# Two attention and expert layers on one core: the second attention's side work placed over whole batches, and two normalizations handed from VectorE to ScalarE

## Chip, core and metric

The kernel runs on one core of a Trainium2 chip. The metric is device time in microseconds (us) of the whole program. TensorE is written PE, VectorE is DVE, ScalarE is ACT, GpSimd is POOL, and SP is the engine that issues most of the DMAs.

## What is computed

Two layers, each a cross attention followed by a mixture of experts, over x of 4 batches, 512 rows and 256 columns, with a context of 4 x 1601 rows. Everything is fp32.

```
x = x + attention0(ctx, layernorm(x))        # 8 heads of 128, context and latents as keys
x = x + experts0(layernorm(x))               # 8 experts, top 2, capacity 512 per expert, gelu (tanh)
x = x + attention1(ctx, layernorm(x))        # 8 heads of 32: q from x, k and v from ctx
x = x + experts1(layernorm(x))               # 8 experts, top 2 by threshold, softmax weights, gelu (erf)

layernorm(x) = (x - mean(x)) / sqrt(var(x) + 1e-5)        # over the 256 columns
attention1:  softmax((q @ Wq.T) (ctx @ Wk.T).T * 32**-0.5) @ (ctx @ Wv.T)
experts1:    logits = x @ Wr + br; keep the two largest; w = softmax(kept)
             out = sum over e of w[e] * (gelu(x @ W1[e] + b1[e]) @ W2[e] + b2[e])
```

## The kernel before

The program has four stages, which follow each other on the one core.

1. First attention, from the start to about 1600 us of the profiled execution.
2. First experts. All eight experts are computed for the first half of their slots and then for the second half (`all_experts`, line 1304). Beside the second half runs `keys_next` (line 1374): keys and values of batch 1 for the second attention, the sum of batch 0's expert results into x (`add_collected`, line 347), the normalized queries of batch 0 (`queries`, line 1128) and its first maxima. `all_experts` takes one piece of this generator at three places of each expert.
3. Second attention, lines 1430 to 1704. There are 16 units, four to a batch: half of the heads (o) by half of the queries (f). A unit goes over the 1601 keys in 13 steps of 128, and the loop at line 1672 takes the steps two at a time. Such a pair of steps is called a pair below, and the steps are numbered 0 to 207, 52 to a batch. In each pair stand, in this order: the scores of two key blocks (`weights`, PE) and their exponentials (line 1476, ACT); the product with the values (`weigh`, PE); one piece of the row maxima of the next unit (`maxima`, PE, and two DVE reductions at line 1205 that read PSUM); the sums of the exponentials (line 1481, DVE); and then whatever the table `at` holds for these steps.
4. Second experts (from line 1709): 8 tiles of 256 rows, one for each expert, and then 13 further tiles from `SURE`, of which the last is short (128 rows). `hidden` is the first layer, `results` the second with the add into the output by an indirect DMA on POOL. The output adds follow one another.

The side work of stage 3 is put into `at` by hand. For batch b, with s0 = 52 b:

- `route2(b - 1)` (line 406): normalizes the finished rows of batch b - 1 for the second experts, chooses experts, counts places, adds the bias product and scatters the rows. It is a generator, and `place` takes one piece of it at each given offset from s0.
- `collect(b + 1)` and `add_collected(b + 1)`: gather the first experts' results on POOL, and add them to x on DVE.
- `queries(b + 1)`: row moments on DVE, a square root on ACT (line 144), five small DVE operations (`ln_scale`), four DVE operations that normalize 128 rows each (line 159), transposes, and two products on PE.
- `projected` (line 1639), for b of 1 and 2: 15 pieces that make keys and values of batch b + 1 on PE, one every two steps, copied out of PSUM by ACT.

PE, DVE, ACT and POOL keep the written order in stage 3 (`in_order(*computing)`, line 1662). SP does not, and neither do the other stages outside the first attention's opening, where a list scheduler orders the instructions; there an instruction is only held by `keep_in_program_order`. In stage 3 all score products, all maxima, and most of the side products share one PSUM pool of three buffers (`c_ps_s`, line 1434); the first side product of a pair takes `c_ps_m`.

[...]

Of the kernel before, what the change touches and what calls it, by code (L numbers as in the profile page):

```python
# [16 lines left out]
P = 128  # L17
# [57 lines left out]
def xattn_ffn_twice(ctx: ExitStack, tc: tile.TileContext, a: dict, out: bass.AP):  # L75
# [61 lines left out]
        nc.vector.tensor_scalar(ve, mv[:, :, 1], EPS, None, ALU.add)  # L137
        return ve

    def ln_root(pool, mv, n, ve=None):  # L140
# [3 lines left out]
        nc.scalar.activation(rs, ve, AF.Sqrt)  # L144
        return ve, rs

    def ln_scale(pool, mv, n, root=None):
# [258 lines left out]
    def route2(b, two, psum, tag, first=0, n=NT):  # L406
# [7 lines left out]
        ve = ln_variance(two, mv, n)  # L414
        yield

        root = ln_root(two, mv, n, ve)
        yield
        mv, rs = ln_scale(two, mv, n, root)
        yield  # L420
        for t in range(n):
            nc.vector.tensor_scalar(
                pay[:, t, :D],
                xb[:, t, :],
                mv[:, t, 0:1],
                rs[:, t : t + 1],
                ALU.subtract,
                ALU.mult,
            )
# [698 lines left out]
    def queries(b, qT):  # L1128
        xn = soon.tile([P, NT, D], F32, tag="xn", name="xn")
        mv = ln_moments(turns, x[b], NT, some=())  # L1130
        for i in range(NT):
            ln_moments(turns, x[b], NT, mv=mv, some=(i,))
            if i + 1 < NT:
                yield
        ve = ln_variance(turns, mv, NT)
        yield

        root = ln_root(turns, mv, NT, ve)
        yield
        mv, rs = ln_scale(turns, mv, NT, root)  # L1140
        for i in range(NT):
            ln_apply(xn, x[b], mv, rs, i)
            if i in (0, NT - 1):
                yield
        xnT = soon.tile([P, DC, S], F32, tag="xnT", name="xnT")
        transposed(banks["beside"], "s", xnT, xn, NT)
        yield
        for o in range(DC):
            ps = banks["beside"].tile([P, 512], F32, tag="s", name="ps_q1")
            for c in range(DC):  # L1150
                nc.tensor.matmul(
                    ps,
                    lhsT=wT[:, 0, c, o * P : (o + 1) * P],
                    rhs=xnT[:, c, :],
                    start=c == 0,
                    stop=c == DC - 1,
                )
            nc.scalar.activation(qT[:, o, :], ps, AF.Copy, scale=DH1**-0.5)
            yield
# [82 lines left out]
    with ExitStack() as st:  # L1242
# [187 lines left out]
    with ExitStack() as st:  # L1430
# [175 lines left out]
        for u in range(1, n_units):  # L1606

            put(NM * u - 7, lambda u=u: negated(u))
            put(NM * u - 5, lambda u=u: to_row(u))
            put(NM * u - 12, lambda u=u: load_queries(u))  # L1610
        for b in range(B):
            s0 = per_batch * b
            if b:
                put(s0 - 10, lambda b=b: load_keys(b, 0))
                put(s0, lambda b=b: load_keys(b, 1))

                beside = (4, 8, 10, 18, 20, 22, 24, 28, 30, 32, 34, 36, 38, 40, 42, 44, 46)
                bare = (4, 8, 10, 12, 12, 14, 14, 16, 18, 20, 22, 24, 26, 28, 30, 32, 34)
                steps = beside if b + 1 < B else bare
                place(s0, route2(b - 1, one, side, "s"), (*steps, *range(steps[-1] + 2, 54, 2), *range(54, 62)))  # L1620
            if b + 1 < B:
                put(s0 + 1, lambda b=b: begin(b + 1))
                got, steps = collect(b + 1)

                for k, f in enumerate(steps):
                    put(max(s0 - 28, 0) + 1 + k, f)
                for t in range(NT):
                    put(
                        s0 + 10 + 2 * t,
                        lambda b=b, got=got, t=t: add_collected(b + 1, got, (t,)),  # L1630
                    )

                def later(b=b):
                    yield from queries(b + 1, qTs[b + 1])

                place(s0, later(), range(12, 32, 2))
            if 1 <= b and b + 1 < B:

                def projected(b=b):
                    *kv, steps = keys_values(side, "s", b + 1, nc.scalar.copy)  # L1640
                    kvs.append(kv)
                    yield
                    for f in steps:
                        f()
                        yield
# [63 lines left out]
    with ExitStack() as st:  # L1709
# [61 lines left out]
            turned_rows(rows, xT, tp)  # L1771
            return xT

        def hidden(w, xT, two=two):
# [345 lines left out]
```

## Time and profile before

| | |
|---|---|
| median of 3 runs | 2819.07 us (2818.01 to 2824.54) |
| the profiled execution | 2825.64 us |
| its span in the profile | 2823.9 us, so 1.7 us lie around it |
| PE busy | 2711.7 us, 96% |
| DVE busy | 1458.4 us, 52% |
| ACT busy | 939.3 us, 33% |
| second attention | from 1914.4 to about 2524 us |
| second experts | from about 2524 us to the end |

Busy time counts an instruction's own duration, and a matmul that runs at a lower clock counts as longer, so a busy PE can still be slow. The granted clock is the share of full speed that PE's clock had in a stretch. A wait names the engine and line that came last before the instruction could begin. The averages hide that the stages have different limits: in the second attention DVE is busy for most of the time, in the experts it hardly is.

### The profile page before, as it was taken

What the parts mean: (1) busy time and instruction counts of PE and PEld (TensorE: products, weight loads), DVE (VectorE), ACT (ScalarE), POOL (GpSimd) and SP (SyncE); (2) the same over time, 40 slices, a digit from 0 to 9 for tenths busy, and PEclk for the clock granted to TensorE, in tenths of its full rate; (3) what the DMA queues carried; (4) which work ended last, traced back from release to release, by engine and by line L of the source; (5) the groups of instructions that cost most, each with busy time, mean ns of one, the idle gap of its engine ahead of it and who ended that gap; (6) DMA issues with size and microseconds to landing.
All of it is one profiled execution on the core that took longest, in us unless ns stands there. A gap on an engine that the chain in (4) does not pass through costs nothing. (4 is left out here: it accounts for less than half of the span.)

```text
span 2823.9 us, 35983 instructions
## 1 busy us (share of the span) xinstructions
PE 2711.7 (96%) x13566; PEld 1853.8 (66%) x13566; DVE 1458.4 (52%) x2307; ACT 939.3 (33%) x1362; POOL 262.4 (9%) x292
## 2 busy tenths in 40 slices
PE   6999999999999999999999999998999998889998
PEld 3667676666666676666676687874454454458887
DVE  6444556544476445455444412137887878872111
ACT  4323234232333233332332211114444444442221
POOL 0000000100001000001000001001110202022542
PEclk9999999999999999999999999999999999999999
DMA  5444343433343433334434555525621111025573
GB/s 172 116 112 116 97 113 86 111 95 92 93 120 89 106 96 95 96 82 107 98 91 125 166 174 172 173 80 156 176 68 40 38 30 56 31 77 188 163 219 103
DMA packets 196435, 311.95 MB, mean 110 GB/s; under 512 B 43319, under 2 KB 117368, under 8 KB 193560
## 3 DMA queue, kind: packets, MB, share of 16 engines
q1 hardware_dynamic: 157512, 227.52, 29.4%
q0 software_dynamic: 14160, 46.31, 5.6%
q10 hardware_dynamic: 24576, 35.68, 4.9%
q8 instruction: 111, 1.82, 0.3%
q14 instruction: 76, 0.62, 0.1%
HBM read 111.73 MB, written 51.34 MB: 58 GB/s over the span
## 5 line engine op out<-in xcount | busy, mean ns | idle before, releaser
L852 DVE TENSOR_REDUCE top<-ps_s 128x1 f32<-128x2113 f32 x128 | 301.8, 2358 | 587.3 <-PE ps_s L844 587.3
L881 PE MATMUL ps_o<-pT,v 128*128 128x256 f32 x2176 | 521.6, 381 | 0.5 <-DVE inv L859 0.5
L844 PE MATMUL ps_s<-kT,qT 128*128 128x512 f32 (+1 forms) x1280 | 489.0, 526 | 5.8 <-ACT attn L858 5.8
L881 PEld LDWEIGHTS ps_o<-pT,v 128*128 128x128 f32 x2176 | 409.9, 191 | 115.2 <-issue 68.4
L858 ACT ACTIVATE attn<-ps_s,top 128x2113 f32<-128x2113 f32 x128 | 259.0, 2024 | 478.8 <-DVE top L852 435.3
L844 PEld LDWEIGHTS ps_s<-kT,qT 128*128 128x128 f32 x1280 | 241.6, 190 | 252.4 <-issue 237.2
L873 DVE STREAM_TRANSPOSE pT<-swapped 128x2176 f32<-128x2176 f32 x128 | 312.4, 2440 | 33.4 <-DMA swapped<-attn 22.7
L1205 DVE TENSOR_REDUCE tops<-ps_s 128x2 f32<-128x1024 f32 (+1 forms) x224 | 238.3, 1105 | 107.4 <-PE ps_s L1194 106.3
L793 PE MATMUL ps_k<-kvin,wkv 128*128 128x512 f32 (+1 forms) x640 | 262.7, 533 | 3.8 <-DVE mv_g L731 2.1
L1463 PE MATMUL ps_w<-asked,keyed 64*128 64x256 f32 (+1 forms) x1664 | 227.8, 408 | 35.0 <-DVE tops L1205 35.0
L827 PE MATMUL ps_v<-wkv,kvin 128*128 128x256 f32 x1088 | 254.6, 381 | 1.3 <-ACT v L834 1.3
L1476 ACT ACTIVATE pT<-ps_w 128x1024 f32<-128x1024 f32 x192 | 189.8, 1022 | 154.1 <-PE ps_w L1463 138.5
L827 PEld LDWEIGHTS ps_v<-wkv,kvin 128*128 128x128 f32 x1088 | 204.7, 190 | 36.8 <-ACT v L834 6.3
L1463 PEld LDWEIGHTS ps_w<-asked,keyed 64*128 64x128 f32 (+1 forms) x1664 | 151.6, 189 | 113.4 <-DVE tops L1205 55.6
L1481 DVE TENSOR_TENSOR sum<-sum,pT 128x1024 f32<-128x1024 f32 x176 | 214.7, 1220 | 13.5 <-PE ps_o L1490 4.9
L806 ACT ACTIVATE kT<-ps_k,bqk 128x512 f32<-128x512 f32 (+1 forms) x160 | 96.8, 620 | 262.9 <-PE ps_k L793 122.4
L793 PEld LDWEIGHTS ps_k<-kvin,wkv 128*128 128x128 f32 x640 | 115.8, 191 | 77.6 <-issue 67.0
L834 ACT COPY v<-ps_v 128x512 f32<-128x512 f32 x144 | 79.7, 560 | 216.6 <-PE ps_v L827 148.3
L1194 PE MATMUL ps_s<-kv,qT 32*128 32x512 f32 (+1 forms) x1024 | 137.0, 561 | 8.8 <-DVE tops L1205 5.1
L1279 PE MATMUL ps_h<-sxT,w 128*128 128x256 f32 x512 | 116.1, 384 | 4.0 <-ACT hT L1286 4.0
L1293 PE MATMUL ps_y<-w,hT 128*128 128x256 f32 x512 | 116.8, 384 | 0.0
L1279 PEld LDWEIGHTS ps_h<-sxT,w 128*128 128x128 f32 x512 | 97.9, 192 | 20.8 <-ACT hT L1286 4.8
(306 smaller groups left out, 2516.1 us busy)
## 6 DMA issues: line engine op xcount, KB each, us to landing
swapped<-attn SPq DMA_DIRECT2D x1536, 68.0 KB
swapped<-attn ACTq DMA_DIRECT2D x512, 68.0 KB
w<-in_w_dram SPq DMA_DIRECT2D x32, 1024.0 KB
rows_b<-empty SPq DMA_DIRECT2D x36, 530.0 KB
w_e<-in_wall_dram SPq DMA_DIRECT2D x5, 2052.0 KB
cw<-in_ctxT_dram SPq DMA_DIRECT2D x4, 1601.0 KB
keyed<-kv SPq DMA_DIRECT2D x32, 200.1 KB
ctx_b<-in_ctx_dram SPq DMA_DIRECT2D x3, 1536.0 KB
```

What stands on the lines that cost most here:

```text
L793: nc.tensor.matmul(ps[:, :n], lhsT=wkv[:, c, hs], rhs=kvin[:, c, : NB - 1, k, :] if k < 4 else kvin[:, c, NB - 1, :, :], start=c == 0, sto ...
L827: nc.tensor.matmul(ps[:, k, :], lhsT=flat_kvin[c][:, j * P : (j + 1) * P], rhs=wkv[:, c, cols], start=c == 0, stop=c == DC - 1,)
L844: nc.tensor.matmul(flat[:, j0 : j0 + n], lhsT=qT[:, t * P : (t + 1) * P], rhs=kT[:, j0 : j0 + n], start=True, stop=True,)
L852: nc.vector.tensor_reduce(top, flat[:, :L], AX.X, ALU.max, negate=True)
L858: nc.scalar.activation(attn[:, :L], flat[:, :L], AF.Exp, bias=top, accum_out=total)
L873: nc.vector.transpose(pT[:, :, k * P : (k + 1) * P].rearrange("p c (a i) -> p a c i", a=4), swapped.rearrange("p a (c i) -> p a c i", i=32),)
L881: nc.tensor.matmul(ps, lhsT=v[:, j - parts[part][0], (h % 2) * DH0 : (h % 2 + 1) * DH0], rhs=pT[:, j, :], start=j == 0, stop=j == NB - 1,)
L1205: nc.vector.tensor_reduce(tops[u][:, t : t + at // n, 2 * pair : 2 * pair + 2, j0 // 512], of, AX.X, ALU.max,)
L1279: nc.tensor.matmul(ps[:, f, :], lhsT=w1[:, c, (f0 + f) * P : (f0 + f + 1) * P], rhs=sxT[:, c, :], start=c == 0, stop=c == DC - 1,)
L1463: nc.tensor.matmul(ps[:r, s, pair * QH : (pair + 1) * QH], lhsT=keyed[o][64 * s : 64 * s + 64, pair, j * P : j * P + r], rhs=asked[u % 3][ ...
L1476: nc.scalar.activation(pT[:r], ps[:r], AF.Exp)
L1481: nc.vector.tensor_tensor(sums[u, 0], sums[u, 0], pT, ALU.add)
```

## The change

Five edits, all in stages 2 to 4.

- `queries` and `route2` no longer normalize on DVE. A new `ln_away` makes -mean x rs with one small DVE operation for four tiles, and a new `ln_apply_scalar` computes rs x + away by an ACT operation with a scale and a bias from SBUF.
- `ln_root` can hold its square root in program order (`behind`): it does so for the queries of batch 0 (stage 2) and the routing of batch 3 (stage 4).
- `keys_next` gives its 15 pieces in groups of four rather than three, so it has three groups before the queries.
- In stage 3 `add_collected` and `queries` of batches 2 and 3 begin 12 steps before the preceding batch begins and take a step's place every two steps (`ask`); those of batch 1 begin at step 10 as before. The 15 pieces of keys and values come one every three steps (offsets 2, 6, 9 ... 48) rather than every two. `route2` is at other offsets.
- In stage 4 the `results` of the last but one tile stand between the two halves of the last tile's `hidden`.

```diff
+    def ln_away(pool, mv, rs, n):
+        away = pool.tile([P, n], F32, tag=f"away{n}", name="away")
+        nc.vector.scalar_tensor_tensor(away, mv[:, :, 0], -1.0, rs, ALU.mult, ALU.mult)
+        return away
+
+    def ln_apply_scalar(dst, src, rs, away, i):
+        nc.scalar.activation(
+            dst, src, AF.Identity, scale=rs[:, i : i + 1], bias=away[:, i : i + 1]
+        )
@@ route2
-        root = ln_root(two, mv, n, ve)
+        root = ln_root(two, mv, n, ve, behind=b == B - 1)
         yield
         mv, rs = ln_scale(two, mv, n, root)
+        away = ln_away(two, mv, rs, n)
         yield
         for t in range(n):
-            nc.vector.tensor_scalar(pay[:, t, :D], xb[:, t, :], ...)
+            ln_apply_scalar(pay[:, t, :D], xb[:, t, :], rs, away, t)
@@ queries
-        root = ln_root(turns, mv, NT, ve)
+        root = ln_root(turns, mv, NT, ve, behind=b == 0)
         yield
         mv, rs = ln_scale(turns, mv, NT, root)
+        away = ln_away(turns, mv, rs, NT)
+        yield
         for i in range(NT):
-            ln_apply(xn, x[b], mv, rs, i)
-            if i in (0, NT - 1):
+            ln_apply_scalar(xn[:, i, :], x[b][:, i, :], rs, away, i)
+            if i % 2:
                 yield
@@ keys_next
-                if k % 3 == 2:
+                if k % 4 == 3:
                     yield
@@ what `at` holds, for b in range(B)
-                beside = (4, 8, 10, 18, 20, 22, 24, 28, 30, 32, 34, 36, 38, 40, 42, 44, 46)
-                bare = (4, 8, 10, 12, 12, 14, 14, 16, 18, 20, 22, 24, 26, 28, 30, 32, 34)
-                steps = beside if b + 1 < B else bare
-                place(s0, route2(b - 1, one, side, "s"), (*steps, *range(steps[-1] + 2, 54, 2), *range(54, 62)))
+                even = (0, 6, 8, 12, 14, 18, 20, 24, 26, 28, 30, 32, 34, 36, 38, 40, 42, *range(44, 62))
+                bare = (0, *range(6, 37, 2), *range(37, 54))
+                place(s0, route2(b - 1, one, side, "s"), even if b + 1 < B else bare)
...
+                first = s0 + 10 if b == 0 else s0 - 12
                 for k, f in enumerate(steps):
-                    put(max(s0 - 28, 0) + 1 + k, f)
+                    put(first - (9 if b == 0 else 14) + k, f)
                 for t in range(NT):
-                    put(s0 + 10 + 2 * t, lambda b=b, got=got, t=t: add_collected(b + 1, got, (t,)))
+                    put(first + 2 * t, lambda b=b, got=got, t=t: add_collected(b + 1, got, (t,)))
-                place(s0, later(), range(12, 32, 2))
+                place(first, ask(b + 1), (0, *range(2, 28, 2)))
             if 1 <= b and b + 1 < B:
-                spread(s0 + 2, projected(), 2, 16)
+                place(s0, project(b + 1), (2, *range(6, 51, 3)))
...
         for f0 in range(0, FC, 2):
+                if f0 == FC // 2:
+                    between()
@@ the loop over the tiles of stage 4
-            hT = hidden(w, xT) if i else first_h
+            if i == 0:
+                hT = first_h
+            elif i < n - 1:
+                hT = hidden(w, xT)
+            else:
+                hT = hidden(w, xT, between=lambda: results(*last))
+                last = None
```

More of the change, by code (lines that the diff above doesn't have):

```diff
@@ L138, in ln_variance, with ln_root @@
         return ve
-    def ln_root(pool, mv, n, ve=None):
+    def ln_root(pool, mv, n, ve=None, behind=False):
         if ve is None:
@@ L143, in ln_root @@
         rs = pool.tile([P, n], F32, tag=f"rs{n}", name="rs")
-        nc.scalar.activation(rs, ve, AF.Sqrt)
+        root = nc.scalar.activation(rs, ve, AF.Sqrt)
+        if behind:
+            tc.keep_in_program_order(root)
         return ve, rs
@@ L415, in route2 @@
         yield
-        root = ln_root(two, mv, n, ve)
+        root = ln_root(two, mv, n, ve, behind=b == B - 1)
         yield
         mv, rs = ln_scale(two, mv, n, root)
+        away = ln_away(two, mv, rs, n)
         yield
         for t in range(n):
[L422 to L429, printed above, removed]
+            ln_apply_scalar(pay[:, t, :D], xb[:, t, :], rs, away, t)
             nc.vector.tensor_scalar(
@@ L1610, in xattn_ffn_twice, with ask, project @@
             put(NM * u - 12, lambda u=u: load_queries(u))
+        def ask(b):
+            begin(b)
+            yield
+            yield from queries(b, qTs[b])
+        def project(b):
+            *kv, steps = keys_values(side, "s", b, nc.scalar.copy)
+            kvs.append(kv)
+            yield
+            for f in steps:
+                f()
+                yield
         for b in range(B):
@@ L1615, in xattn_ffn_twice @@
                 put(s0, lambda b=b: load_keys(b, 1))
[L1617 to L1620 removed]
+                even = (0, 6, 8, 12, 14, 18, 20, 24, 26, 28, 30, 32, 34, 36, 38, 40, 42, *range(44, 62))
+                bare = (0, *range(6, 37, 2), *range(37, 54))
+                place(s0, route2(b - 1, one, side, "s"), even if b + 1 < B else bare)
             if b + 1 < B:
[L1622 removed]
                 got, steps = collect(b + 1)
+                first = s0 + 10 if b == 0 else s0 - 12
                 for k, f in enumerate(steps):
[L1626 removed]
+                    put(first - (9 if b == 0 else 14) + k, f)
                 for t in range(NT):
                     put(
[L1629 removed]
+                        first + 2 * t,
                         lambda b=b, got=got, t=t: add_collected(b + 1, got, (t,)),
                     )
[L1633 to L1636 removed]
+                place(first, ask(b + 1), (0, *range(2, 28, 2)))
             if 1 <= b and b + 1 < B:
[L1639 to L1645, printed above, removed]
[L1647 removed]
+                place(s0, project(b + 1), (2, *range(6, 51, 3)))
         put(per_batch * (B - 1) + 4, load_first_weights)
@@ L1772, in turned, with hidden @@
             return xT
-        def hidden(w, xT, two=two):
+        def hidden(w, xT, two=two, between=lambda: None):
             n = xT.shape[-1]
```

## The prediction

> **What bounds the kernel now.** I read the page's busy shares and slices first, then the second attention unit by unit in the table by windows, then PE's timeline around each change for its idle times, and ACT's timeline for what had caused them. The first lines are the page's, the next a table by windows (busy us of PE, weight loads, DVE, ACT and POOL, with their instructions, then PE's granted clock, DMA share and GB/s), the rest timelines (start us, us, engine, line, operation, idle time before and its releaser).
>
> ```profile
> PE 2711.7 (96%) x13566; PEld 1853.8 (66%) x13566; DVE 1458.4 (52%) x2307; ACT 939.3 (33%) x1362; POOL 262.4 (9%) x292
> PE   6999999999999999999999999998999998889998
> DVE  6444556544476445455444412137887878872111
> ...
> 2022.30:2053.70 31.40, 29.54 (x303) 15.31 (x297) 28.00 (x29) 15.28 (x19) 0.40 (x4) 1.00 0.72 195
> 2053.70:2091.70 38.00, 36.13 (x321) 18.77 (x323) 32.62 (x41) 19.88 (x26) 0.20 (x2) 1.00 0.31 76
> 2091.70:2133.80 42.10, 41.51 (x343) 25.42 (x341) 37.35 (x63) 21.62 (x31) 11.22 (x16) 1.00 0.14 35
> 2133.80:2179.00 45.20, 42.72 (x347) 22.96 (x347) 32.12 (x49) 19.57 (x29) 0.00 (x0) 1.00 0.13 43
> 2179.00:2219.90 40.90, 33.02 (x321) 18.29 (x315) 37.15 (x75) 15.81 (x20) 9.70 (x9) 0.98 0.15 40
> 2346.90:2389.10 42.20, 35.34 (x323) 18.92 (x317) 36.17 (x74) 15.80 (x20) 10.15 (x9) 0.92 0.14 34
> ...
> 1760.62 0.20 ACT L144 ACTIVATE rs<-ve 128x4 f32<-128x4 f32 x1 [4.32 <-DVE ve L137]
> 1762.79 3.78 PE L1279 MATMUL ps_h<-sxT,w 128*128 128x256 f32 x8 [3.72 <-ACT hT L1286]
> 1911.11 3.64 PE L1463 MATMUL ps_w<-asked,keyed 64*128 64x256 f32 x16 [2.54 <-DVE tops L1205]
> 2537.45 1.11 PE L1404 MATMUL tp<-ident,cw 128*128 128x128 f32 x4 [4.06 <-ACT cw L1421]
> ```
>
> PE is the bound nearly everywhere. In the second attention PE and DVE take turns: the six windows are units 3 to 7 and 11. Unit 6 is PE's (42.7 of 45.2 us busy, DVE 32.1); unit 7 is DVE's (37.2 of 40.9, PE 33.0), and so is 11. Two neighbours with opposite limits are what a better spread could gain from. The last four lines show single stalls: in the first experts a square root on ACT waits 4.3 us for its variance, with the gelus behind it, so PE stands for 3.7 us; in the second experts the same instruction delays the last gelu by which PE's next PSUM bank comes free, 4.1 us.
>
> **Stage 2, the square root: -5 us.** The list of instructions by engine shows ACT's root of batch 0 moved from behind the second half's first gelu to behind its twelfth. Its variance, ready at 1760.6, is then long there. The wait of 3.72 goes. The eight matmuls after it took 3.78 us, and eight of the 32 at full clock take 7.07 / 4 = 1.77, so the stall also cost 2.0 by a lowered clock. I take 5 of 5.7. What comes instead on ACT: table load 1.28, root 0.20, six small DVE operations near 0.2 each, four rows at 0.5 (overlapped), table load 1.28, some 6 us together, between two groups of gelus that lie 8.5 us apart, during a `results` of 7.07. Hidden; without that cover 6 us would come back.
>
> **The turn into stage 3: -1 us.** Three groups of keys instead of five and one more yield in `queries` bring the maxima one place forward, so the last piece now stands ahead of the last `results`, and its two reductions (2.36) no longer keep the first scores waiting 2.54. But two pieces of maxima now follow with only a transposition between, and share the same two banks: where the trace has a transposition between such a pair, PE waits 0.73; here I take 1.1. The copy of the last y (0.69) may hold PE in place of the reductions, if banks are handed over all at once. 2.54 - 1.1 - 0.4 gives 1.
>
> **Stage 3.** DVE loses 16 rows of queries and 16 of routing in the program, 24 of them in this stage: 24 x 0.408 = 9.8 us, and gains six `away` at 0.17. ACT gains 24 rows; the nearest row is the same operation in the first attention's opening, `ctx_b<-ctx_b,away,rs`, at 585 ns: 14.0 us.
>
> [...] But ACT is busy 15 to 22 us of units of 31 to 45, DVE 28 to 37, so what counts is DVE's 8.8 us, and of that only the part in pairs that DVE limits.
>
> The rest is moved. Prices per piece, from the timeline of unit 6 and its neighbours: PE two key blocks of scores 2.0, their product with the values 1.04, a piece of maxima 1.1, keys 1.85, values 1.87, a transposed batch 1.05, half the queries 1.85, the logits 1.9; DVE two reductions 2.27, two sums 2.5, one collected tile 1.0, its moments 0.6, and the routing's small operations 0.2 each. I laid these out over the 104 pairs by the two tables of offsets, and took the larger of PE and DVE (or ACT, in a few pairs) in each. Before, steps 80 and 82 hold keys, half the queries and the routing's transposes or logits together: PE 10.0 and 10.4, DVE 4.2 and 6.7. After: PE 5.2 and 6.6, DVE 3.5 and 6.8. Over the stage:
>
> - larger of the two in each pair: 593.6 before, 586.6 after, -7;
> - larger of the two in each unit, as if DVE and PE could run a whole unit apart: 557.2 before, 558.5 after, +1.
>
> By batches the first reads +2.5, -3, -7, +1: units 3 and 7 receive eight collected tiles (8 x 0.48) and four moments (4 x 0.6), and both were DVE's; that gives back what units 5, 6, 9, 10 and 11 win. The trace has 609.6 (1914.4 to 2524.0), nearer to the first sum, as three PSUM buffers let PE run only about one pair ahead; but unit 6's measured 41.7 us for six pairs against 44.6 by the sum shows some carrying over. I take -4, and -9 to +5 as ends.
>
> Waits that are added: the rows on ACT wait for `away`, and the next exponentials stand behind them. `away` is made two steps earlier, so the wait is DVE's lag. Before, the transposition on PE waited for DVE's row instead (0.34). Nothing moves late by DMA: the gathers of batch 2 stand on POOL at the same steps but for one, behind the clearing of rows, and the last was issued at 2016.7, with a median of 6.5 us to landing; `add_collected` for it now comes near 2040 rather than 2098. The load of the context for batch 3 now waits for keys that end at step 100 rather than 84, and stands on SP behind eight small weight loads, whose buffers are free from step 98. Keys begin at step 110, ten steps or some 27 us later, in a stretch with a DMA share near 0.15. Without that slack its 1.6 MB would stand on the path, near 10 us.
>
> **The clock.** In windows of 4 us, the clock falls to 0.66 at 1912 to 1916 after the wait of 2.54, to 0.69 at 1960 after 2.33, to 0.68 at 2357 after 2.05, and to 0.58 at 2409 after 2.39: a lowered stretch costs near 1.7 us (4 x 0.34 + 4 x 0.09 at the first). [...] Of ten such stretches in the stage, two are in unit 11, which becomes lighter, and up to two may come in unit 3 and 7. Net nothing in the sum, 3 us either way in the range.
>
> **Stage 4: -4 us.** The root now stands behind all gelus of the first tile. The gelu that ran at 2536.6 can run as soon as its products end, 2533.4, so 4.06 becomes about 0.9. Then two table loads, the root, the DVE chain behind a copy and three rows, about 6 us, stand before the next tile's gelus, near 2540.4; three PSUM buffers (`d_ps_h`) take PE to about 2541.3. Covered, but barely: I take back 0.5 for the last row and the copies, and add 0.5 for the clock (these 32 matmuls took 8.81 where others take 7.07). About -3. At the end `results` of the last but one tile (7.07) start before half of the last tile's first layer (1.8). Its output adds were issued at 2804.50 and 2809.04, the last at 2813.45; the adds follow each other at 4.4 to 4.5. The first can go at about 2803.2, when the add before it is done, and the chain ends 1.2 earlier. Together -4.2.
>
> **The sum.** -5 - 1 - 4 - 4.2 = -14 against the profiled 2825.64, so 2811. The median of the runs lies 6.6 below that execution; the same subtraction gives 2805.
>
> **Rivals.** About 0.3% (8.5 us) is what a measurement of this kernel can tell from no change.
>
> 1. The single stalls go, and stage 3 gives nothing: the sum by units holds, units 3 and 7 turn fully DVE's and lower the clock. -5 - 1 - 4 + 3 = -7: 2812, within the bound. For it: DVE's 28.0 of 31.4 in unit 3. Against: the 609.6 near the first sum. Chance 0.17.
> 2. The sum by pairs holds in full, and evened pairs also end most lowered stretches (five of ten, 1.7 each) and both experts' clock losses: -5.7 - 2.5 - 7 - 8 - 4 = -27: 2792. For it: PE's waits on `tops` in units 7, 11 and 12, up to 2.4 us each. Against: those same units receive work. Chance 0.23.
> 3. Slower. ACT keeps its order, so a row that waits for `away`, or a root that waits for its variance, holds the exponentials, and these the three PSUM buffers. There are six such chains in the stage with two waits each. If DVE lags by a pair's two reductions and two sums, each wait costs up to 2.4 us of PE and half of them a lowered stretch: 12 x (2.4 + 0.9) = 40, less 14: about +20, 2838 with half of it 2822. It decides once DVE is more than about a pair behind ACT when the row comes. For it: at 2114.88 the exponentials already waited 1.0 us on a small DVE operation. Against: after that root PE waited 0.59, after the one at 2088 not at all. Chance 0.08.
>
> That the work is not spread can be left out: the list shows the keys, queries and routing pieces at the new places, and both rows on ACT.
>
> **How the numbers follow.** The forecast has 0.52. Faster: forecast and rival 2, 0.75. Same: rival 1, 0.17. Slower: rival 3, 0.08. The range runs from rival 2's 2792, less 2, to 2819, which takes in rival 1 and stage 3's worse end (+5 for -4).
>
> **What would show it.** PE's waits of 3.7 on hT in stage 2 and 4.1 on cw in stage 4 gone; unit 6 and 10 below 43 us, unit 3 above 35; DVE's busy time lower by some 12 us, ACT's higher by some 18, with no more table loads; output adds ending about 1 us sooner against the last products. I am wrong if ACT shows waits on `away` with PE waiting on pT behind them, if units 3 and 7 grow by more than 5, 6, 9 and 10 shrink, or if the context of batch 3 comes late.

## The result, and the profile after

| | before | after |
|---|---|---|
| median of 8 runs each, same chip | 2819.36 us (2816.81 to 2824.54) | 2812.71 us (2804.51 to 2819.02) |
| ratio after / before | | 0.9968, 95% interval 0.9956 to 0.9980 |
| the profiled execution | 2825.64 us | 2812.18 us |

The ratio, with its interval, means -9.0 us (-5.6 to -12.4): faster, by less than the 14 us forecast. The two medians in the table are 6.7 us apart, which lies inside that interval. A second measurement on another chip (`e0_after` below) gave 0.9971, or -8.2 us. The two profiled executions differ by 13.5 us, because the one of before lies 6.3 us above its median and the one of after 0.5 us below its own. A difference of two traces shows where time went; it does not show how much of it every run keeps.

First the page's busy rows and slices of after:

```profile
PE 2704.5 (96%) x13566; PEld 1846.9 (66%) x13566; DVE 1447.4 (52%) x2283; ACT 955.2 (34%) x1394; POOL 260.6 (9%) x292
PE   6999999999999999999999899998989899989998
DVE  6544556544476444445444421136887878973111
```

DVE has lost 11.0 us (12 expected), ACT gained 15.9 (18). The work was handed over as described. What that did to the units can be read in the table by windows for units 3, 4, 5, 6, 7 and 11 of after (busy us of PE, weight loads, DVE, ACT and POOL, then PE's clock, DMA share, GB/s):

```profile
2017.70:2054.30 36.60, 29.52 (x299) 15.44 (x293) 33.91 (x47) 17.66 (x23) 1.49 (x6) 1.00 0.67 179
2054.30:2097.20 42.90, 40.86 (x314) 20.38 (x315) 33.98 (x47) 22.37 (x31) 12.28 (x17) 0.92 0.29 73
2097.20:2136.00 38.80, 38.00 (x347) 22.25 (x341) 30.81 (x41) 20.26 (x30) 0.00 (x0) 1.00 0.12 28
2136.00:2174.50 38.50, 37.12 (x335) 21.96 (x335) 29.88 (x54) 17.33 (x24) 0.00 (x0) 1.00 0.01 3
2174.50:2222.40 47.90, 41.33 (x339) 20.85 (x338) 40.26 (x79) 20.59 (x27) 16.85 (x16) 0.96 0.30 90
2340.90:2385.20 44.30, 42.18 (x337) 21.13 (x335) 33.87 (x62) 17.66 (x24) 18.34 (x16) 0.92 0.17 49
```

Unit 6 fell from 45.2 to 38.5 and unit 5 from 42.1 to 38.8. Units 3 and 7 rose from 31.4 to 37.1 and from 40.9 to 47.9, with DVE busy for 33.9 and 40.3 us of them. The single stalls are in the timelines (start us, us, engine, line, operation, idle time before it and its releaser). ACT in stage 2, after the change:

```profile
1796.97 1.28 ACT L145 ACT_TABLE_LOAD   x1
1798.27 0.20 ACT L145 ACTIVATE rs<-ve 128x4 f32<-128x4 f32 x1
1799.71 2.07 ACT L173 ACTIVATE xn<-x,away,rs 128x256 f32<-128x256 f32 x4 [1.24 <-DVE away L168]
```

The root finds its variance ready, and PE has no wait on hT in that half. PE at the turn into stage 3 and at its end:

```profile
1905.07 2.00 PE L1473 MATMUL ps_w<-asked,keyed 64*128 64x256 f32 x16 [0.87 <-DVE y L1311]
1909.61 1.78 PE L1204 MATMUL ps_s<-kv,qT 32*128 32x512 f32 x4 [1.48 <-ACT sum L1486]
...
2513.29 1.45 PE L1414 MATMUL tp_f<-ident,cw 128*128 128x128 f32 x4 [4.82 <-DMA cw<-rows_a]
2514.66 1.94 PE L1500 MATMUL ps_o<-pT,kv 128*32 128x256 f32 x16
...
2527.49 0.66 PE L1414 MATMUL tp<-ident,cw 128*128 128x128 f32 x4 [0.93 <-ACT cw L1431]
```

The wait of 4.06 on cw is 0.93 now. New is the 4.82 at `tp_f`: PE has come to the end of the attention and stands there for the first tile's rows of stage 4. The four transpositions after it took 1.45 us (0.66 before) and the product with the values 1.94 (1.07 elsewhere), so the clock was lowered too (granted clock 0.50 from 2512.5 to 2516.5). POOL and SP around that moment, after the change:

```profile
2508.46 1.02 POOL L560 DMA_INDIRECT rows_a<-pay,place_a  x1 [0.30 <-issue]
2509.92 0.98 POOL L560 DMA_INDIRECT rows_b<-pay,place_b  x1 [0.44 <-DMA rows_b<-pay,place_b]
2510.60 2.00 SPq L1590 DMA_DIRECT2D cw<-rows_a  x4
```

And before it:

```profile
2507.46 0.98 POOL L552 DMA_INDIRECT rows_a<-pay,place_a  x1 [0.30 <-issue]
2510.24 2.15 SPq L1580 DMA_DIRECT2D cw<-rows_a  x4
2516.28 1.72 POOL L552 DMA_INDIRECT rows_a<-pay,place_a  x1 [4.54 <-DMA cw<-rows_a]
```

The load goes out at the same time in both, 2510. It brings the rows of the first two tiles. Before, it stood ahead of the last quarter of batch 2's sends, POOL waited for it, and PE came to `tp_f` only at 2522.2. After, all sixteen scatters stand ahead of it, and PE is there at 2508.5. The whole second attention (first exponential to the end of the last copy of oT) reads 609.9 before and 608.5 after; up to the moment when PE is ready for `tp_f` it reads 607.8 and 599.9.

### The profile page after: what moved, and what is told of

Read it like the earlier page. It is cut to its first block, busy times and chain, and to the rows that moved or that the text cites. A ratio compares the mean times of both kernels' runs of the same rounds, so it can differ in the third digit from the quotient of the medians.

```text
span 2810.5 us, 36014 instructions
## 1 busy us (share of the span) xinstructions
PE 2704.5 (96%) x13566; PEld 1846.9 (66%) x13566; DVE 1447.4 (52%) x2283; ACT 955.2 (34%) x1394; POOL 260.6 (9%) x292
## 5 line engine op out<-in xcount | busy, mean ns | idle before, releaser
L1204 PE MATMUL ps_s<-kv,qT 32*128 32x512 f32 (+1 forms) x1024 | 136.0, 554 | 10.7 <-DVE tops L1215 7.3
L1303 PEld LDWEIGHTS ps_y<-w,hT 128*128 128x128 f32 x512 | 96.3, 190 | 17.3 <-issue 3.9
```

The lines of the kernel that those rows point to most:

```text
L1303: nc.tensor.matmul(ps[:, t, :], lhsT=hT[:, f, t * P : (t + 1) * P], rhs=w2[:, f, :], start=f == 0, stop=f == FC - 1,)
```

## Experiments

Each was timed beside before on the same chip, and the difference in us is (ratio - 1) times the median of before there. "Stage 3" is read from each trace, first exponential to the end of the last copy of oT. Runs with the same letter shared a chip. On A, before itself was slower (median 2832.69) than on the others (2819.86 to 2822.42).

| chip | run | ratio (95%) | us | stage 3 |
|---|---|---|---|---|
| A | e1_holds | 0.9969 (0.9959 to 0.9978) | -8.8 | 619.5 |
| A | e2_old_places | 1.0002 (0.9990 to 1.0014) | +0.6 | 632.7 |
| A | e3_rows_dve | 0.9982 (0.9969 to 0.9994) | -5.1 | 620.0 |
| A | e4_early_sends | 0.9931 (0.9918 to 0.9945) | -19.5 | 603.8 |
| B | e0_after | 0.9971 (0.9961 to 0.9981) | -8.2 | 609.9 |
| B | e6_rows_apart | 0.9962 (0.9949 to 0.9975) | -10.7 | 604.8 |
| B | e7_slow_clears | 0.9955 (0.9939 to 0.9971) | -12.7 | 604.5 |
| B | e8_later_ask | 0.9962 (0.9947 to 0.9976) | -10.7 | 611.7 |
| C | e5_rows_ahead | 0.9931 (0.9917 to 0.9944) | -19.5 | 595.9 |
| C | e9_back_ask | 0.9948 (0.9934 to 0.9961) | -14.7 | 605.0 |
| C | e10_late_sends | 0.9941 (0.9928 to 0.9955) | -16.6 | 603.6 |
| D | e12_together | 0.9934 (0.9920 to 0.9949) | -18.6 | 599.7 |

**e1_holds: the held roots alone, put into the kernel before.**

```diff
-        nc.scalar.activation(rs, ve, AF.Sqrt)
+        root = nc.scalar.activation(rs, ve, AF.Sqrt)
+        if behind:
+            tc.keep_in_program_order(root)
```

> The kernel before, with only the square roots of batch 0's queries (stage 2) and of batch 3's routing (stage 4) held in program order; all rows stay on VectorE, groups of keys stay three to a group, stage 3 and the tail as before. Theory: these two single stalls are worth their length and the lowered clock after them, so the 3.7 us wait on hT and the 4.1 us wait on cw go: stage 2 -5, start of stage 4 -3, together about -8 us (ratio 0.997). Rival: the roots only move the wait: with the rows of the queries still on VectorE and queued behind its other work, the chain root, scale, rows, transposition holds the last gelus of the first experts or the first scores of stage 3, and the sum is -3 to 0 us. The trace tells: PE's wait before the eight ps_h matmuls of stage 2, the time from the last ps_y of stage 2 to the first exponential (7.0 before), and PE's wait on cw at the start of stage 4.

It measured -8.8 us, the theory's -8. PE's timeline has neither stall left; the first experts' 32 products run through, and cw is waited for 0.93:

```profile
1753.85 7.07 PE L1281 MATMUL ps_h<-sxT,w 128*128 128x256 f32 x32
...
2536.88 0.66 PE L1406 MATMUL tp<-ident,cw 128*128 128x128 f32 x4 [0.93 <-ACT cw L1423]
```

The rows were still on DVE here, so the held roots do not need the other edits. By the ratios they carry as much as the whole change, though the two ratios come from different chips. The trace shows more: from the first key products beside the second half of stage 2 (1743.48 in before) to the first exponential of unit 1 it takes 193.5 us, where before takes 203.4, and stage 4 takes 294.4 instead of 299.6. That is 15.1 us against one execution of before, which lies 6.3 us above its median.

The same stretch settles what the turn is worth. The twelve traces that have the change's other edits of stage 2 too (e3's with the rows still on DVE) read 197.5 to 198.1 there, three of them on e1's chip. They run the same matmuls as e1, and take 4.0 us longer; e1 is one trace, but the twelve lie within 0.6 us of each other. So it is the other order of the pieces that costs this, and not the rows. PE at the turn, in e1 and then in e4 on the same chip:

```profile
1904.57 3.21 PE L1465 MATMUL ps_w<-asked,keyed 64*128 64x256 f32 x16 [2.54 <-DVE tops L1207]
```

```profile
1887.29 2.53 PE L1204 MATMUL ps_s<-kv,qT 32*128 32x512 f32 x8 [1.05 <-DVE tops L1215]
1889.76 8.54 PE L1303 MATMUL ps_y<-w,hT 128*128 128x256 f32 x32
...
1907.35 2.00 PE L1473 MATMUL ps_w<-asked,keyed 64*128 64x256 f32 x16 [0.88 <-DVE y L1311]
...
1911.89 1.13 PE L1204 MATMUL ps_s<-kv,qT 32*128 32x512 f32 x4 [1.49 <-ACT sum L1486]
```

The wait of 2.54 is gone and 0.88 and 1.49 stand in its place. What is new besides is the wait of 1.05 at two neighbouring pieces of maxima, with eight matmuls that take 2.53 where a piece without such a wait takes 1.14, and a clock of 0.68 from 1890 to 1894 behind it, in which the 32 products take 8.54 for 7.17.

**e2_old_places: the changed kernel with the old table, the rows in one pair with `away`.**

```diff
-                place(first, ask(b + 1), (0, *range(2, 28, 2)))
+                place(s0, later(), (12, 14, 16, 18, 20, 22, 22, 24, 26, 28, 30, 32))
...
-                bare = (0, *range(6, 37, 2), *range(37, 54))
+                bare = (4, 8, 10, 12, 12, 14, 14, 16, 18, 20, 22, 24, 26, 28, 30, 32, 34)
```

> The changed kernel, with stage 3's table of places put back to that of before (the extra piece of the queries stands in the same pair as the one before it); rows on ScalarE, the held roots, groups of four and the tail stay changed. Theory A (places earn stage 3's gain, and the end of stage 3 loses it again to the late scatters): from the first exponential to the last oT copy about 609 us as before, no wait on cw<-rows_a, total about 1 us over the changed kernel. Theory B (VectorE's shorter list earns it, the places give nothing): about 602 us, and since the old places have no wait on the rows at the end, total 5 to 7 us under the changed kernel. In between, each has its share of the 8 us by which PE came earlier to the end of the stage.

It was neither theory's number: +0.6 us against before, although both held roots and the tail were in it. By the medians it is 10.4 us over e1 on the same chip. Its trace shows rival 3 of the prediction. ACT's waits on DVE, from the view of the tile away (us, times), and then the timelines of ACT and of PE behind the longest of them:

```profile
  DVE away L168: 24.0, 6
```

```profile
2448.47 1.09 ACT L173 ACTIVATE pay<-x,away,rs 128x256 f32<-128x256 f32 x2 [7.08 <-DVE away L168]
2449.46 1.00 ACT L1486 ACTIVATE pT<-ps_w 128x1024 f32<-128x1024 f32 x1
...
2450.52 2.08 PE L1204 MATMUL ps_s<-kv,qT 32*128 32x512 f32 x4 [3.94 <-ACT pT L1486]
```

In these tables the small DVE operations that end in `away` and the first two rows fall into the same pair of steps. DVE comes to them only behind the pair's reductions and sums; ACT is already there, keeps its order, and stands 4.5 to 7.1 us with the exponentials behind it. PE's waits on pT are 11.8 us in stage 3, where before has 1.2.

**e6_rows_apart: the same, but with a pair of steps between `away` and the rows.**

```diff
-                place(s0, later(), (12, 14, 16, 18, 20, 22, 22, 24, 26, 28, 30, 32))
+                place(s0, later(), range(12, 36, 2))
-                bare = (4, 8, 10, 12, 12, 14, 14, 16, 18, ...)
+                bare = (4, 8, 10, 12, 14, 14, 14, 16, 18, ...)
```

> The kernel of the old places with rows on ScalarE, but the rows one pair of steps behind away (queries: one piece every pair from offset 12 on; routing of batch 2: away at 12, rows at 14), as in the changed kernel. Theory: what made the old places with rows on ScalarE cost some 10 us was ScalarE, waiting 4.5 to 7.1 us for away with the exponentials behind it, because away and the first rows stood in one pair; with a pair between them ScalarE waits at most 2.3 us, PE's waits on pT (3.0, 1.5, 1.5 and 3.9 us) go, and the total is 8 to 12 us under that kernel: about 0.997 of before, equal to the changed kernel. Rival: it is the rows' own time on ScalarE that counts, or the places themselves: then the total stays within 4 us of before.

The theory held. The total is 11 us under e2 by their ratios, each against before on its own chip, and the same view reads:

```profile
  DVE away L168: 6.5, 4
```

PE's waits on pT are 1.2 us, as before. Two more readings follow. The rows on ACT at the old places bring stage 3 from 609.9 to 604.8 in the traces. It is not one lucky trace: units 1, 2, 6, 9, 10, 12 and 13 read the same in before and in e1, to 0.1, and together they are 4.8 us shorter here. And this kernel, with none of the new placing in stage 3 beyond that one pair, is not slower than the changed kernel on the same chip (0.9962 against 0.9971, intervals overlapping): as the change has it, the new placing earned nothing.

**e3_rows_dve: the new places, the rows back on DVE.**

```diff
-            ln_apply_scalar(xn[:, i, :], x[b][:, i, :], rs, away, i)
+            ln_apply(xn, x[b], mv, rs, i)
```

> The changed kernel, with the rows of queries and of routing normalized by VectorE again (tensor_scalar with mean and rs, no away); places, held roots and tail stay changed. Theory A (places earn stage 3's gain): PE is ready for tp_f some 600 us after the first exponential as in the changed kernel, total within 2 us of it. Theory B (VectorE's list earns it): ready 6 to 8 us later; part of it disappears in the wait on the rows (4.8 us), so the total is 1 to 4 us over the changed kernel. Third: the waits of ScalarE on away (12 us in all in the changed kernel) cost PE time: then this kernel is faster by 2 us or more.

It measured -5.1 us, less than the held roots alone give on that chip (-8.8), and 3 us over what the changed kernel measured elsewhere. That speaks for theory B, that the shorter list of DVE matters. Its trace can't size it as a whole, since DVE stands for 6.89 us in unit 11, which the profile puts down to "remote" and to no instruction, and PE stands 3.61 us with it. But units 8, 13 and 14, which take 39.7, 34.5 and 33.5 us in after's first trace, in e0 and in e5 alike, take 41.9, 36.9 and 35.9 here.

**e0_after: the changed kernel itself, on the chip of e6 to e8.**

> The changed kernel itself, unchanged, so that its stages can be compared on the same chip as the experiments. Theory: total 0.997 of before; PE waits some 5 us at tp_f on cw<-rows_a; and where the profiles of the experiments show a wait of 4 to 7.5 us on asked<-qT at the end of unit 3 (the first queries of batch 1), this one shows 3 to 5 us of it too, since it comes from the clearing of rows, which is the same in all. Rival: that wait belongs to the edits of those experiments; then it is absent here, as in the first profile of the changed kernel.

The ratio came again, 0.9971. PE waited 5.95 at `tp_f`. There was no wait on asked<-qT in unit 3, so my theory of that wait was wrong as far as it said "in all". It appears in all four traces of chip A (3.9 to 7.5 us) and in none of the other chips, before's and after's first profiles included. In e4, SP's timeline shows it behind the clearing of rows:

```profile
2048.43 1.20 SPq L409 DMA_DIRECT2D rows_b<-empty  x2
2049.73 1.00 SPq L1121 DMA_DIRECT2D keyed<-kv  x1
2050.83 3.45 SPq L1180 DMA_DIRECT2D asked<-qT  x4
```

In the first trace of after, the same load goes out at 2040.69. Stage 3 had begun 2.3 us earlier there, so the load is some 8 us late in e4. It stands behind the clears in the kernel before as well; why A was later with them is not settled.

**e4_early_sends: batch 2's sends four pairs of steps earlier.**

```diff
-                bare = (0, *range(6, 37, 2), *range(37, 54))
+                bare = (0, *range(6, 29, 2), *range(29, 54))
```

> The changed kernel, with the routing of batch 2 closer together after its logits (offsets 6 to 28 by two and then every step, instead of 6 to 36 by two and then every step), so that its eight sends stand about four pairs of steps, some 11 us, earlier. Theory: PE's wait of 4.8 us at tp_f on the rows (and the lowered clock of the products after it, some 2 us) comes from the sixteen scatters that stand ahead of the load; it goes: last oT copy and all that follows 5 to 7 us earlier, ratio to before about 0.9945. Rival 1: the routing's VectorE work in units 13 and 14 lengthens these by as much (units 12 to 14 102 us in the changed kernel), total within 2 us of it. Rival 2: another thing holds tp_f (the bank or ScalarE's queue), PE still waits about 5 us there.

No wait at `tp_f` is left, and the ratio, 0.9931, is even better than the theory's. Its chip is the one with the late loads of asked, of which e4 itself shows 3.9 us and e1 7.5, so part of the -19.5 may be a smaller share of that delay; without a trace of before there, this stays open. The same edit gives only -12.7 on another chip (e7). Rival 1 holds in part: unit 14 went from 33.5 to 38.7, with PE waiting 3.2 on a DVE addition of the routing.

**e7_slow_clears: e4, and the clearing of rows three steps apart.**

```diff
-                put(4 + k, f)
+                put(4 + k // 2 * 3, f)
```

> The changed kernel with the earlier sends of batch 2, and the clearing of rows put three steps apart for each two pieces instead of two. Theory: on SP the clears wait for each other some 7 us where a pair of steps lasts 5.3, so they fall behind, and the loads of asked for batch 1 behind them come late: PE's wait of 3.9 us on asked<-qT and the lowered clock after it go, total 4 to 6 us under the kernel with the earlier sends alone (ratio to before 0.991 to 0.9915). Rival: the transfers themselves are slow (DMA share 0.8), and the wait stays within 1 us of 3.9; or the clears now delay the loads of unit 5 and 6 by as much.

Inconclusive for the clears, as that chip showed no late load of asked to begin with. Against e0 on the same chip it gives -4.5 us by ratio for the earlier sends, and stage 3 604.5 against 609.9, so the routing in unit 14 takes back some of the wait that is removed.

**e5_rows_ahead: only the load of the first rows 14 steps earlier.**

```diff
-        put(NM * n_units - 6, load_first_rows)
+        put(NM * n_units - 20, load_first_rows)
```

> The changed kernel with the load of the first tile's rows (load_first_rows) 14 steps earlier, at step 188, ahead of the sends of batch 2; nothing else moves. The first tile of the second experts is therefore computed without the rows that batch 2 sends. Theory: the wait of 5 to 6 us at tp_f is the load standing behind sixteen scatters and nothing else; it goes with the lowered clock after it, units stay, the last oT copy comes 5 to 7 us earlier after the first exponential (603 to 605 us instead of 610), total 0.995 of before. Rival: PE's time before tp_f, freed, is given back by something else that was late too (first weights, ScalarE's copies of oT): less than 2 us under the changed kernel.

The theory held as to the wait, and more came than it said: -19.5 us against before, 11 under the changed kernel by ratios (0.9931 against 0.9971). Unit 15 fell from 31.2 in e0 to 23.3, which is the wait and its lowered clock, 7.9 us. PE passes without a wait:

```profile
2500.30 0.65 PE L1414 MATMUL tp_f<-ident,cw 128*128 128x128 f32 x4
```

Stage 3 is 595.9, 14.0 under before's 609.9. Another 6.2 of the difference to e0 lies in units 6 and 7, where nothing was edited; the next lines show why. They are units 7 of e0 and of e4 in windows of 4 us:

```profile
2194.70:2198.70 4.00, 3.46 (x14) 2.23 (x13) 3.83 (x8) 0.00 (x0) 2.05 (x2) 0.77 0.33 104
2198.70:2202.70 4.00, 3.32 (x6) 0.74 (x4) 3.86 (x11) 0.59 (x1) 2.38 (x3) 0.50 0.36 87
2202.70:2206.70 4.00, 4.00 (x20) 2.69 (x24) 0.32 (x1) 1.25 (x2) 1.92 (x2) 0.50 0.54 178
```

```profile
2196.00:2200.00 4.00, 3.69 (x48) 2.29 (x44) 3.66 (x16) 1.64 (x2) 2.70 (x3) 1.00 0.13 40
2200.00:2204.00 4.00, 3.13 (x10) 1.43 (x10) 3.86 (x7) 0.59 (x1) 2.15 (x2) 1.00 0.34 98
2204.00:2208.00 4.00, 3.34 (x36) 2.01 (x40) 2.60 (x8) 2.05 (x2) 1.96 (x2) 1.00 0.50 127
```

The clock is the third column from the right. The same instructions, with nearly the same waits (0.54 and 0.68 us in e0, 0.50 and 0.68 in e4), run at half clock in one execution and at full clock in the other. Unit 7 took 51.5 and 51.6 us in two traces (e0 and e7) with two lowered stretches, 47.9 in after's first with one, and 46.2 in e4 with none.

**e8_later_ask and e9_back_ask: e7 with the collected tiles and queries of batches 2 and 3 begun later.**

```diff
-                first = s0 + 10 if b == 0 else s0 - 12
+                first = s0 + 10 if b == 0 else s0 - 4       # e8
+                first = s0 + 10                             # e9, gathers 36 steps ahead of it
...
-                place(s0, project(b + 1), (2, *range(6, 51, 3)))
+                place(s0, project(b + 1), (2, *range(4, 49, 3)))       # e9
```

> The kernel with earlier sends and slower clears, and with collected tiles and queries of batches 2 and 3 beginning 4 steps before the preceding batch instead of 12. Theory of the prediction (units 3 and 7 became VectorE's by the eight collected tiles and four moments): unit 7 falls from 46 to some 41 us, unit 3 by 2 to 3, units 4 and 8 rise by less, total 3 to 5 us under the kernel without this. Rival: the work only moves: units 3 and 4 together, and 7 and 8 together, stay within 1 us, total within 2 us.

> The kernel with earlier sends and slower clears, but collected tiles and queries of batches 2 and 3 begin at step 10 of the preceding batch, as before the change (their gathers too), while the 15 pieces of keys and values stay one every three steps, two steps earlier (4, 7 ... 46), and the routing stays at the new offsets. Theory (larger of PE and VectorE in each pair, summed as in the prediction): 583.4 against 586.3 for the kernel that it is made from, and unit 7 is VectorE's no more: unit 7 from 51.6 to some 43, unit 3 from 37 to 31.4, units 5 and 9 up by 2 to 4: total 3 to 6 us under that kernel, ratio to before about 0.994. Rival: what counts is that the queries of a batch are out of the way of the routing and keys (the run with these at s0 - 4 was no faster than at s0 - 12): total 0 to 5 us over that kernel.

Both did to units 3 and 7 what was said: 37.1 to 31.4, and 51.6 to 43.2 and 41.1. Both gave it back elsewhere: unit 5 from 38.8 to 44.4 and 47.9, unit 9 from 38.8 to 44.4 and 43.8. Against e7, e8 is 7 us worse in the trace and not to be told apart by ratios; e9 is the same in both. The sum of the larger engine in each pair had put e9 at -2.9, and no such gain shows.

**e10_late_sends: e7 with the sends of batches 0 and 1 six steps later.**

```diff
-                even = (..., 38, 40, 42, *range(44, 62))
+                even = (..., 38, 40, 42, *range(50, 68))
```

> The kernel with earlier sends and slower clears, and the last 18 pieces of the routing of batches 0 and 1 (its sends first) at offsets 50 to 67 instead of 44 to 61, so that most of them fall out of units 7 and 11 into 8 and 12. Theory: unit 7 holds one pair of sends and small operations too many for VectorE; with 3 us less of VectorE's work there PE's waits on tops and the two lowered stretches of its clock (0.50 at 2198 to 2206) go, unit 7 falls from 51.6 to 45 or less, units 8 and 12 rise by 1 to 2: total 3 to 5 us less. Rival: the pairs that hold unit 7 up are those of the collected tiles at its beginning, before the sends: unit 7 stays above 46, total within 2 us.

Unit 7 is 45.2 and at full clock; unit 8 rose from 39.7 to 43.4. Stage 3 is 603.6 against 604.5, and the ratios can't be told apart.

**e12_together: the rows ahead, slow clears and late sends at once.**

> The changed kernel with three edits: the load of the first tile's rows ahead of the sends of batch 2 (which the first tile then leaves out), the clearing of rows three steps apart, and the sends of batches 0 and 1 at offsets 50 on. Theory: the three add up where they act at different places: 0.9931 of before with the rows ahead, and some 2 to 4 us less by unit 7 (46.9 in that run, 45.2 with late sends) and by a load of asked that cannot come late: ratio 0.992. Rival: the late sends only move work into units 8 and 12 (43.4 instead of 39.7 for unit 8), so with PE no longer waiting for the rows nothing more is won: ratio 0.993 to 0.994.

The rival was right: 0.9934, equal to e5's 0.9931. With PE not waiting for the rows, the later sends won nothing more. e5, e12 and e4 have the lowest ratios of all. But in e5 and e12 the rows of the first two tiles are loaded ahead of all that batch 2 sends, which these tiles then leave out; in the kernel before the last quarter of the sends comes too late for them, in the changed kernel none. Among those that send all rows first, e4 and e10 have the lowest ratios (0.9931 and 0.9941), each on a chip on which the changed kernel itself was not timed.

## Why the prediction was right, and where it was not

| term | predicted | first traces | what the runs add |
|---|---|---|---|
| stage 2, root | -5 | -5.0, with the new wait of the turn in it | both roots -8.8 by e1's ratio (-6.2 to -11.6); in its trace -9.9 up to unit 1 |
| turn into stage 3, with unit 0 | -1 | -0.9 | +4.0, counted from e1's trace |
| stage 3 from unit 1 | -4 | -3.1 | by the ratios -3 (within 5 either way); wait at `tp_f` +7 to +8 |
| stage 4, start | -3 | -2.7 | in e1's |
| stage 4, rest | -1.2 | -3.5 | |

The rest of the traces' difference is a stage 1 that ran 1.7 us longer. The -3 by the ratios is -9.0 for the whole less e1's -8.8, the turn's +4.0 and the tail's -1.2; it joins two chips and one stretch of traces. The same sum gives -4.7 for e6 and -13.5 for e5, where their traces have -5.1 and -14.0 in stage 3.

**The held roots** were right in mechanism; in size they were worth about the -8 of the sum by the ratio, and 7 us more in the trace. The places where their waits went were right: ACT hides the table loads, the root and the rows in stage 2 between the gelus, and at the start of stage 4 the cover just sufficed (0.93 left, as forecast). Of the 3.5 in the rest of stage 4, 1.2 is the tail as forecast (16.9 to 15.8 us from the start of the last tile's first layer to the issue of the last add) and 1.7 the first 32 products, which took 7.15 us instead of 8.81; I had put only 0.5 on that clock.

**The turn** is a step that failed, in sign. The wait of 1.1 between two pieces of maxima came as forecast (1.06), and so did the wait on the last y (0.87 for 0.4). I had put nothing on the eight slower matmuls behind that first wait (1.1 us more: the trace of before has them at 2.26 instead of 1.14 behind such a wait, at 1850.80), nothing on one more lowered stretch of the clock (about 1.7 us, the price that I had used in stage 3; in the first trace it came in unit 0, which grew by that much), and had not seen that in unit 0 PE would wait 1.48 for the first sum on ACT, behind its table load. The last products and the first exponential are nearer to each other (7.0 to 4.4), but the stretch as a whole is 4.0 longer than with the roots alone. That the two terms of stage 2 and the turn, -6 together, match the first traces' -5.9 is luck: in the traces the roots gave more, and the turn took it back.

**Stage 3: the step that failed is "Nothing moves late by DMA".** I followed the gathers and the context's load past their queues, but not the sends of batch 2, which the new `bare` table puts one to a step, all ahead of `load_first_rows`. The load's own time did not change (2510); PE came 13.8 us earlier in absolute time and ran into it. In the sum this is +6.9 us in the first trace: 4.82 of wait and some 2.1 for the transpositions, values and first-layer products at a lowered clock (1.45 for 0.66, 1.94 for 1.07, 4.19 for 3.72). e5 moves the load and nothing else, and unit 15 loses 7.9.

The gain ahead of it was larger than my -4. Up to `tp_f` PE won 7.9 in the first trace, 9.6 without unit 0; that is nearer to the sum by pairs (-7) than to the sum by units (+1). Which edit earned it can be told in part. The rows on ACT, at old places and a pair behind `away`, gave 5 in the trace of e6. New places with rows on DVE were not faster than before, beyond what the roots give (e3). Both together without the wait at the end gave 14 in the trace of e5, but that kernel leaves rows out, and 4.6 of its 14 us under e0 is unit 7's clock. Between places, e8, e9 and e10 show work moving from unit to unit with no clear change of the sum. The sign named for a failure did not come: units 3 and 7 grew by 12.6 in the first traces, and 5, 6, 9 and 10 shrank by 18.2.

**The rows on ScalarE.** The prediction let DVE's shorter list outweigh the longer row on ACT. e6 bears that out here: the row takes 592 ns on ACT, against 408 on DVE in before, and stage 3 is 5 us shorter (604.8 against 609.9). What e2 adds is that the price of this was not the row: it was 11 us for one missing pair of steps. Rival 3 described this, with its chance of 0.08 and its figure of 2.4 us for a wait, though its sum does not come out: 40 less 14 is 26, not 20, which makes 2845. The change escapes it because the rows stand a pair of steps behind `away`, and ACT then waits at most 2.3 us.

**The clock.** "Net nothing in the sum, 3 us either way" held in the first traces: (1 - granted clock) over windows of 4 us of stage 3 comes to 20.7 us before and 22.2 after. But a price of 1.7 us for each stretch was too orderly: in e0's unit 7 the lowered windows lose (0.23 + 0.50 + 0.50) x 4 = 4.9 us beside PE waits of 0.54 and 0.68, and in e4 waits of 0.50 and 0.68 lose nothing. So in these two traces the length of a wait did not decide whether the clock fell beside it; what did, no run shows.

**From trace to median.** The sum of -14 against the profiled 2825.64 gave 2811, and the profiled after was 2812.18. The step to the median, "the same subtraction gives 2805", failed: by the ratio the change is -9.0, and the median is 2812.7. The first profile of before lies 6.3 us above its median, and a term read from it is worth less in the median: against that trace e1's is 15.1 us shorter in the two stretches read above, and e1's ratio gives 8.8. The executions of before that took longer have the lower clock (on chip D 0.988 at 2814.26 us and 0.983 at 2825.85; on chip A a mean of 2825.1 us at 0.987, 2832.8 at 0.983 and 2837.3 at 0.981), which fits; which stages hold the 6.3 can't be told from one trace. So 2812.7 lands on rival 1's number. Rival 1's ground, that stage 3 gives nothing, is not shown (-3 within 5), and its reason was not right: units 3 and 7 did fill up with DVE's work (33.9 and 40.3 us busy), yet moving it out of them (e8, e9) did not help, and moving the rows to ACT did.

## What to carry to other kernels

When an engine is made to arrive earlier, list every transfer that it meets at the end of the stage, with its issue time and what stands ahead of it on POOL and SP; most of a gain of 8 us was lost to one load whose time had not moved. When work goes to an engine that keeps the written order, put at least one round of the loop between the instruction that makes its operand and its first use; here that was the difference between 0.9962 (e6) and 1.0002 (e2). A single trace places a stall but does not size the change: compare it with the median first. And a sum that comes right does not clear its terms: only a run with one of them alone showed that the turn had the wrong sign.

## What was not expected of the hardware

- The same instructions, with waits under 1 us, ran at a clock of 0.50 for some 8 us in one execution (e0, 2198.70 to 2206.70) and at 1.00 in another (e4); unit 7, 46.2 us in e4, varied by 5.4 us along with it.
- On one chip, the load behind the clearing of rows on SP came some 8 us later than on the first (asked<-qT at 2050.83 in e4 against 2040.69 in after, less 2.3), and PE waited 3.9 to 7.5 us for it in all four traces there; before was 10 to 13 us slower on that chip. The cause is not settled.
- After the change, a scatter of 128 rows kept POOL busy for 0.98 to 1.90 us, but sixteen of them, written one pair to a step, took 27 us (2483.44 to 2510.90), with waits up to 2.6 us on the scatters ahead of them.
